# Graph attention, then nucleus diffusion, on one core: the first layer's row work moved between the next chunk's products, and a pair's exponentials placed ahead of a copy-out

## The chip, the core and the metric

The kernel runs on one core of a Trainium2 chip, as one program with one launch. The metric is the device time of the whole program in microseconds (us). Three runs of the kernel before took 3929.79, 3929.95 and 3939.95 us, median 3929.95 us. The profiled execution took 3928.85 us, with a span of 3926.9 us in its trace and a mean granted TensorE clock of 0.938.

The engines are called PE (TensorE: matrix products and transposes), DVE (VectorE), ACT (ScalarE), POOL (GpSimd) and SP (SyncE, which here only issues loads and stores). Each works through its own queue in order.

## The reference, cut to what matters

There are N = 2708 nodes with 512 features, in 22 row tiles of 128 (the last has 20 rows). Everything is float32.

```python
h = relu(layernorm(x))                                    # layer 0: graph attention, 8 heads of 64
feats = einsum('nf,hfd->hnd', h, W)
attn  = softmax(leaky(e_self[:, :, None] + e_neigh[:, None, :]) + mask(adj))
x1    = x + relu(einsum('hnm,hmd->hnd', attn, feats) + b) # heads side by side
v     = relu(layernorm(x1))                               # layer 1: two diffusion steps on v
S = adj + I;  Rf = S by its row sums, Rb = S by its column sums
Xf = Xb = Xa = v;  Z = 0
for s in range(2):
    A  = nucleus_softmax((Xa @ W1) @ W2 @ (Xa @ W3).T)    # per row the largest to 0.9 of the mass
    Xf, Xb, Xa = Rf @ Xf, Rb @ Xb, A @ Xa
    Z += Xf @ U1[s] + Xb @ U2[s] + Xa @ U3[s]
out = x1 + layernorm(v + Z) * gamma + beta
```

(In the reference layer 1 is called with the adjacency matrix as its S.) What matters here: x1 is the output of layer 0; from it come v, the "keys" and "queries" of step 0 (two small projections of v), and a copy of v split into a high and a low part for the products with S.

## The kernel before, in words

**Layer 0.** A first loop over the 22 tiles makes the features `fw`, and the exponentials of the neighbour terms as one row per head, stored in `en_d`. Then the output columns are worked through in six chunks: five of 512 nodes and one of 148. Per chunk, the 22 tiles `a_c` of the transposed adjacency matrix are loaded (L275); ACT sums and converts each (L280) and it is stored into `s_d` as S. For two groups of four heads, and for each of the 22 tiles, DVE makes four tiles `e` (L295, ring of 10) and PE adds each into `po` with one float32 product, which the trace shows as two records (L297). ACT copies the sums to `o_t` (L300). Row sums of the adjacency matrix (`arow`, one buffer, L259 to L260) also run on ACT, four loads per chunk, as early as the buffer allows.

After a chunk's products, each of its tiles is turned back (L313, PE), divided by its sum (L314 to L324, DVE and POOL), gets bias, ReLU and the residual (L325, L326), and is stored as `x1_d` and, with beta added, as `xb_d` (L327 to L329). DVE and PE run this right at the start of the next chunk.

When all chunks are done, W1, W2 and W3 are loaded and combined into `kw` (L351 to L364). Then a loop over 22 tiles (L855 to L864) reloads x1, normalizes it (L137 to L146), clears negatives on POOL (L860) into `va`, splits it (L833, L834, on DVE) into `vhl_d`, turns it on PE (L152), projects it (`project`, L372, eight records per tile), and stores keys and queries in `kq_d` (L378 to L386, ACT and POOL).

Outside the diffusion steps' main part the order of the queues is chosen by the scheduler of the tile framework, from the order of the source and its own estimates.

**Diffusion steps.** In each step (s = 0 and 1) the order on PE, ACT, DVE and SP is the order of the source. Rows are worked in 11 pairs of tiles. `Logits.products` (L440) makes a pair's scores in PSUM, ACT copies them to `p` (L442). `Logits.exp` takes the row maxima (L467, DVE), two exponentials per tile on ACT (L472, L479), a dozen small steps on POOL (`points`, L484 to L495), and 12 passes over `p` on ACT (the "looks", L472). `search` (DVE) narrows the threshold in rounds (L547), calls `early` after its first round and `late` before its last part (`finish`), which makes the kept scores `keep` (L648). Then `attended` turns `keep` on PE (L944) and multiplies by `va` (L963), and `mixed` applies U1, U2, U3 (L991).

S's products run beside this. `part` gives the steps of one half of a quad of tiles: loads of `hl` and `s_r` (L893, L895), products (L899), and at the end `scaled`, which copies the sums out on ACT (L905), stores them, and in step 0 splits them on DVE (L833, L834).

A loop over g from -1 to 10 joins these. At g = -1 nothing can be attended yet. `early` fills the list `fills` with pair 1's exponentials and looks, and `late` runs

```python
paced(others, len(others))     # the second half of S's first products, and their scaled copies
for step in fills:             # then pair 1's exponentials and looks
    step()
```

so that on ACT the exponentials stand behind the copies of S's products. In step 1, `va` is loaded from `xa_d` before everything (L871), and `ranks` counts ties on DVE (L1059) with `spread` (L1065 to L1069) called before the loop.

Of the kernel before, what the change touches and what calls it, by code (L numbers as in the profile page):

```python
# [53 lines left out]
def kernel(  # L54
# [43 lines left out]
    x1_d = dram.tile([N, D], F32, name="x1_d")  # L98

    xb_d = dram.tile([N, D], F32, name="xb_d")  # L100
    y_d = dram.tile([N, D], F32, name="y_d")
# [41 lines left out]
    def layernorm(pool, src, dst, pr):  # L143

        mean, rs = moments(pool, src, pr)
        nc.vector.tensor_scalar(dst, src, mean, rs, op0=OP.subtract, op1=OP.mult)  # L146

    def transposed(pool, psum, src, pr, name):

        pt = psum.tile([P, KD, P], F32, name="t")  # L150
        for k in range(KD):
            nc.tensor.transpose(pt[:, k, :pr], src[:pr, k * P:(k + 1) * P], ident[:pr, :pr])  # L152
        dst = pool.tile([P, KD, P], F32, name=name)
        nc.scalar.copy(dst[:, :, :pr], pt[:, :, :pr])  # L154
        return dst

# [11 lines left out]
    nchunks = [(c, min(c + 512, N)) for c in range(0, N, 512)]  # L168
    with ExitStack() as l0:
# [8 lines left out]
        cpart = big.tile([P, NT, len(nchunks)], F32, name="cpart")  # L178
# [4 lines left out]
        with tc.tile_pool(name="l0w", bufs=1) as wp, tc.tile_pool(name="l0p", bufs=2) as pp, \  # L183
# [9 lines left out]
            for i, vec in enumerate((a_self, a_neigh)):  # L193
                v_b = pp.tile([P, D], F32, name="v_b")
                nc.sync.dma_start(out=v_b, in_=row_bcast(vec, D))
                for k in range(KD):
                    prod = pp.tile([P, D], F32, name="prod")
                    nc.vector.tensor_mul(prod, w_sb[:, k, :], v_b)
                    nc.vector.tensor_reduce(wa[:, k, i * H:(i + 1) * H],
                                            prod.rearrange("p (h d) -> p h d", h=H),  # L200
                                            axis=AX.X, op=OP.add)
            hs = wp.tile([P, KD, NT], F32, name="hs")
            r_t = wp.tile([H, N], F32, name="r_t")
            for t in range(NT):
# [4 lines left out]
                layernorm(pp, xt[:pr], h[:pr], pr)  # L209
# [42 lines left out]
        small = l0.enter_context(tc.tile_pool(name="l0small", bufs=3))  # L252
        ps_o = l0.enter_context(tc.tile_pool(name="l0pso", bufs=6, space=PSUM))
# [10 lines left out]
        for ci, (n0, n1) in enumerate(nchunks):  # L264
            cw = n1 - n0
            tiles = [t for t in range(NT) if n0 <= t * P < n1]
            r_b = rbp.tile([P, H, 512], F32, name="r_b")
            nc.sync.dma_start(
                out=r_b[:, :, :cw],
                in_=bass.AP(tensor=en_d.tensor, offset=en_d.offset + n0, ap=[[0, P], [N, H], [1, cw]]))  # L270
            a_c = []
            for t in range(NT):
# [4 lines left out]
                wide = min(512, NT * P - n0)  # L277
# [8 lines left out]
            for t in tiles:  # L286
                row_sums(t)
            o_t = work.tile([DV, H, 512], F32, name="o_t", bufs=1)
            for grp in hgroups:
                po = [ps_o.tile([DV, 512], F32, name="po") for _ in grp]  # L290
                for t in range(NT):
                    pr = rows[t]
                    for i, hd in enumerate(grp):
                        e = tp.tile([P, 512], F32, name="e")
                        nc.vector.scalar_tensor_tensor(e[:pr, :cw], r_b[:pr, hd, :cw], kk[:pr, t, hd:hd + 1],  # L295
                                                       a_c[t][:pr, :cw], op0=OP.max, op1=OP.mult)
                        nc.tensor.matmul(po[i][:, :cw], lhsT=fw[:pr, t, hd, :], rhs=e[:pr, :cw],  # L297
                                         start=(t == 0), stop=(t == NT - 1))
                for i, hd in enumerate(grp):
                    nc.scalar.copy(o_t[:, hd, :cw], po[i][:, :cw])  # L300
            for t in tiles:
                pr = rows[t]
                c0 = t * P - n0
                xt = work.tile([P, D], F32, name="xt0")
                nc.sync.dma_start(out=xt[:pr], in_=x[cols[t], :])
                o = work.tile([P, D], F32, name="o")
                o3 = o.rearrange("p (h d) -> p h d", h=H)
                den = small.tile([P, H], F32, name="den")
                pos = []
                for g, grp in enumerate(hgroups):  # L310
                    pn = ps_t.tile([P, HG, DV], F32, name=f"pn{g}")
                    for i, hd in enumerate(grp):
                        nc.tensor.transpose(pn[:pr, i, :], o_t[:, hd, c0:c0 + pr], ident[:DV, :DV])  # L313
                    nc.vector.tensor_scalar(den[:pr, grp[0]:grp[-1] + 1], pn[:pr, :, DH],  # L314
                                            lone_n[:pr, t:t + 1], None, op0=OP.add)
                    pos.append(pn)
                rden = small.tile([P, H], F32, name="rden")
                nc.vector.reciprocal(rden[:pr], den[:pr])
                for pn, grp in zip(pos, hgroups):
                    s = slice(grp[0], grp[-1] + 1)  # L320
                    nc.vector.scalar_tensor_tensor(
                        o3[:pr, s, :], fsum.rearrange("p (h d) -> p h d", h=H)[:pr, s, :],
                        lone[:pr, t:t + 1], pn[:pr, :, :DH], op0=OP.mult, op1=OP.add)
                nc.gpsimd.tensor_mul(o3[:pr], o3[:pr], rden[:pr].unsqueeze(2).to_broadcast([pr, H, DH]))  # L324
                nc.gpsimd.tensor_add(o[:pr], o[:pr], b_b[:pr])  # L325
                nc.vector.scalar_tensor_tensor(o[:pr], o[:pr], 0.0, xt[:pr], op0=OP.max, op1=OP.add)  # L326
                nc.gpsimd.dma_start(out=x1_d[cols[t], :], in_=o[:pr])  # L327
                nc.gpsimd.tensor_add(xt[:pr], o[:pr], beta_b[:pr])
                nc.gpsimd.dma_start(out=xb_d[cols[t], :], in_=xt[:pr])  # L329
# [17 lines left out]


    kw = const.tile([P, KD, 2 * DA], F32, name="kw")
    with tc.tile_pool(name="w12", bufs=1) as wp, tc.tile_pool(name="w12ps", bufs=1, space=PSUM) as ps:  # L350
        nc.sync.dma_start(out=kw[:, :, :DA], in_=w3.rearrange("(k p) a -> p k a", p=P))  # L351
        w1_sb = wp.tile([P, KD, DA], F32, name="w1_sb")
        w2_sb = wp.tile([DA, DA], F32, name="w2_sb")
        w1_t = wp.tile([DA, KD, P], F32, name="w1_t")
        nc.sync.dma_start(out=w1_sb, in_=w1.rearrange("(k p) a -> p k a", p=P))
        nc.sync.dma_start(out=w2_sb, in_=w2)
        pw_t = ps.tile([DA, KD, P], F32, name="pw_t")
        for k in range(KD):
            nc.tensor.transpose(pw_t[:, k], w1_sb[:, k], ident)
        nc.scalar.copy(w1_t, pw_t)  # L360
        pw = ps.tile([P, KD, DA], F32, name="pw")
        for k in range(KD):
            nc.tensor.matmul(pw[:, k], lhsT=w1_t[:, k], rhs=w2_sb, start=True, stop=True)
        nc.scalar.copy(kw[:, :, DA:], pw)  # L364

    def project(pool, psum, v_t, t, s):


        pr = rows[t]
        pk = psum.tile([P, KD, P], F32, name="t")  # L370
        for k in range(KD):
            nc.tensor.matmul(pk[:, 0, :pr], lhsT=kw[:, k, :], rhs=v_t[:, k, :pr],  # L372
                             start=(k == 0), stop=(k == KD - 1))
        big = pool.tile([P, P], F32, name="kq_b")
        hl = pool.tile([P, 2, P], F32, name="kq_hl")
        if pr < P:
            nc.gpsimd.memset(hl, 0.0)
        nc.scalar.copy(hl[:, 1, :pr], pk[:, 0, :pr])  # L378
        nc.scalar.mul(big[:, :pr], pk[:, 0, :pr], 4097.0)


        high, x = hl[:, 0, :pr], hl[:, 1, :pr]
        nc.gpsimd.tensor_tensor(high, big[:, :pr], x, op=OP.subtract)
        nc.gpsimd.tensor_tensor(high, big[:, :pr], high, op=OP.subtract)
        nc.gpsimd.tensor_tensor(x, x, high, op=OP.subtract)
        nc.gpsimd.dma_start(out=kq_d[s][:, :, t * P:(t + 1) * P], in_=hl)  # L386
# [440 lines left out]
    def split_rows(pool, x, t, to):  # L827

        pr = rows[t]
        hl = pool.tile([P, 2, D], F32, name="split_hl")  # L830
        if pr < P:
            nc.vector.memset(hl, 0.0)
        nc.vector.tensor_scalar(hl[:pr, 0].bitcast(I32), x.bitcast(I32), -4096, None, op0=OP.bitwise_and)  # L833
        nc.vector.tensor_tensor(hl[:pr, 1], x, hl[:pr, 0], op=OP.subtract)  # L834
        nc.gpsimd.dma_start(out=to[t * P:(t + 1) * P], in_=hl)

    for s in range(STEPS):
        last = s == STEPS - 1
        with ExitStack() as st:
# [14 lines left out]
            if not last:  # L854
                for t in range(NT):  # L855
                    pr = rows[t]
                    x1 = work.tile([P, D], F32, name="yo")
                    nc.sync.dma_start(out=x1[:pr], in_=x1_d[cols[t], :])
                    layernorm(small, x1[:pr], va[:pr, t, :], pr)
                    nc.gpsimd.tensor_scalar(va[:pr, t, :], va[:pr, t, :], 0.0, None, op0=OP.max)  # L860
                    split_rows(parts, va[:pr, t, :], t, vhl_d)
                    v_t = transposed(work, ps_t, va[:, t, :], pr, "v_t")
                    project(small, ps_t, v_t, t, s)
# [4 lines left out]
            rank = big.tile([P, N], BF16, name="rank") if last else None  # L868
            if last:
                for t in range(NT):  # L870
# [294 lines left out]
```

## Time and profile before

The span by stage, read with the view of busy time by windows:

| stage | from, to (us) | what sets its end |
|---|---|---|
| features | 0 to 190 | PE, ACT, POOL in turn |
| chunks 0 to 4, 512 wide | 190 to 997 | PE, about 163 us for a chunk |
| chunk 5, 148 wide | 997 to 1067 | PE and DVE |
| last rows, kw, normalize and project | 1067 to 1237 | a chain over POOL, DVE, PE, ACT |
| step 0 up to the first attended pair | 1237 to 1391 | see the prediction |
| step 0, 11 pairs | 1391 to 2475 | PE |
| step 1 up to the first attended pair | 2475 to 2702 | see the prediction |
| step 1, 11 pairs | 2702 to 3927 | PE |

PE is busy for 3436.3 us of the span, DVE for 2647.5, ACT for 1530.8 and POOL for 792.2. In a timeline row the columns are start, length, engine, line, operation, output and inputs, count; the bracket says how long the engine stood idle before the row and what ended that. A window row gives each engine's busy time in that stretch, then the granted PE clock, the DMA share and GB/s.

### The profile page before, as it was taken

The numbers are of one execution on the slowest core, as the hardware profiler recorded it, in microseconds if no ns is written. First come the engines' busy times: TensorE is split into PE (matmuls) and PEld (weight loads), VectorE is DVE, ScalarE is ACT, GpSimd is POOL, SyncE is SP. The second block draws the span as 40 slices with busy tenths as digits, with TensorE's granted clock in tenths as the row PEclk, the third lists the DMA queues.
The fourth block names the chain that finished last, engine by engine and source line by source line (L and its number), as shares of the span: only waits on it lengthen the run. The fifth ranks groups of instructions, "written<-read, shape, count | busy, mean of one in ns | idle before, by whom it ended". The sixth has DMA issues, their size and how long they took to land. (4 is left out here: it accounts for less than half of the span.)

```text
span 3926.9 us, 35723 instructions
## 1 busy us (share of the span) xinstructions
PE 3436.3 (88%) x11313; PEld 1789.7 (46%) x11313; DVE 2647.5 (67%) x4839; ACT 1530.8 (39%) x2306; POOL 792.2 (20%) x1183
## 2 busy tenths in 40 slices
PE   7998999999745289898989899775999999999988
PEld 4432333333534255554545444353566555566543
DVE  3388898998843644646464552596779977777992
ACT  1243202011012466564656551217545654445511
POOL 3213111020265102122121211301111212112101
PEclk9999999999856799999999999897999999999999
DMA  2377424231145525355454543781676555676652
GB/s 74 101 261 256 130 72 148 67 102 39 39 159 169 179 97 204 134 172 188 148 178 147 185 152 106 236 266 65 211 244 204 203 196 200 210 235 204 209 191 81
DMA packets 276027, 634.10 MB, mean 161 GB/s; under 512 B 36937, under 2 KB 63453, under 8 KB 272803
## 3 DMA queue, kind: packets, MB, share of 16 engines
q1 hardware_dynamic: 248751, 540.99, 41.9%
q0 software_dynamic: 27024, 90.30, 6.0%
q8 instruction: 91, 1.49, 0.2%
q14 instruction: 161, 1.32, 0.1%
HBM read 509.07 MB, written 122.10 MB: 161 GB/s over the span
## 5 line engine op out<-in xcount | busy, mean ns | idle before, releaser
L963 PE MATMUL a<-va,at 128*128 128x512 f32 (+2 forms) x1936 | 888.3, 597 | 10.4 <-ACT at L948 10.2
L297 PE MATMUL po<-e,fw 128*65 128x512 f32 (+3 forms) x2112 | 838.4, 557 | 22.7 <-DVE e L295 22.5
L899 PE MATMUL q<-hl,s_r 128*128 128x512 f32 x2904 | 819.9, 428 | 34.6 <-DMA s_r<-s_d 34.4
L295 DVE SCALAR_TENSOR_TENSOR e<-r_b,kk,a_c 128x512 f32<-128x512 f32 (+3 forms) x1056 | 756.2, 741 | 98.2 <-PE po L297 25.1
L899 PEld LDWEIGHTS q<-hl,s_r 128*128 128x128 f32 x2904 | 543.3, 189 | 278.9 <-issue 131.8
L472 ACT ACTIVATE junk_a<-p,nth 128x2708 uint8<-128x2708 f32 (+1 forms) x240 | 613.0, 2554 | 90.4 <-POOL nth L492 86.8
L297 PEld LDWEIGHTS po<-e,fw 128*65 128x65 f32 (+1 forms) x2112 | 282.5, 141 | 555.0 <-issue 295.6
L991 PE MATMUL a<-u_k,v_t 128*128 128x512 f32 (+1 forms) x1056 | 491.4, 601 | 20.6 <-ACT xa L971 15.2
L963 PEld LDWEIGHTS a<-va,at 128*128 128x128 f32 (+2 forms) x1936 | 336.3, 186 | 373.9 <-issue 340.1
L547 DVE SCALAR_TENSOR_TENSOR junk<-p,th 128x2708 bf16<-128x2708 f32 (+1 forms) x132 | 402.4, 3049 | 4.0
L440 PE MATMUL t<-keys,q_t 128*128 128x452 f32 x528 | 170.7, 452 | 200.6 <-ACT p L442 184.9
L948 ACT COPY at<-t 128x512 f32<-128x512 f32 (+3 forms) x308 | 140.0, 476 | 439.8 <-PE t L944 439.5
L991 PEld LDWEIGHTS a<-u_k,v_t 128*128 128x128 f32 (+1 forms) x1056 | 188.5, 187 | 240.6 <-issue 186.5
L723 DVE SCALAR_TENSOR_TENSOR keep<-p,th 128x2708 f32<-128x2708 f32 (+1 forms) x44 | 133.4, 3033 | 148.1 <-PE t L944 147.0
L440 PEld LDWEIGHTS t<-keys,q_t 128*128 128x128 f32 x528 | 93.7, 215 | 273.2 <-ACT p L442 242.0
L833 DVE TENSOR_SCALAR split_hl<-xe 128x512 int32<-128x512 int32 (+1 forms) x44 | 19.0, 432 | 267.3 <-ACT xe L905 212.6
L725 DVE MAX8 vn<-keep 128x8 f32<-128x2708 f32 (+1 forms) x66 | 196.8, 2981 | 2.3
L280 ACT ACTIVATE s_c<-a_c 128x512 fp32r<-128x512 f32 (+2 forms) x132 | 76.2, 577 | 256.1 <-DMA a_c<-in_adj_t_dram 115.8
L442 ACT COPY p<-t 128x452 f32<-128x452 f32 (+2 forms) x264 | 133.0, 539 | 108.4 <-PE t L440 72.1
L154 ACT COPY v_t<-t 128x512 f32<-128x512 f32 (+1 forms) x154 | 80.9, 570 | 227.2 <-PE t L152 221.4
L944 PE MATMUL t<-ident,keep 128*128 128x128 f32 (+1 forms) x968 | 147.0, 274 | 24.1 <-DVE keep L675 16.0
L944 PEld LDWEIGHTS t<-ident,keep 128*128 128x128 f32 (+1 forms) x968 | 115.1, 139 | 103.8 <-issue 75.7
(275 smaller groups left out, 3220.2 us busy)
## 6 DMA issues: line engine op xcount, KB each, us to landing
s_r<-s_d SPq DMA_DIRECT2D x330, 256.0 KB
hl<-vhl_d SPq DMA_DIRECT2D x132, 512.0 KB
u_k<-in_L_gnn_U_dram SPq DMA_DIRECT2D x264, 256.0 KB
hl<-fhl_d SPq DMA_DIRECT2D x132, 512.0 KB
hl<-bhl_d SPq DMA_DIRECT2D x132, 512.0 KB
arow<-in_adj_dram SPq DMA_DIRECT2D x21, 1354.0 KB
s_d<-s_c SPq DMA_DIRECT2D x110, 256.0 KB
a_c<-in_adj_t_dram SPq DMA_DIRECT2D x105, 256.0 KB
```

The lines of the kernel that those rows point to most:

```text
L295: nc.vector.scalar_tensor_tensor(e[:pr, :cw], r_b[:pr, hd, :cw], kk[:pr, t, hd:hd + 1], a_c[t][:pr, :cw], op0=OP.max, op1=OP.mult)
L297: nc.tensor.matmul(po[i][:, :cw], lhsT=fw[:pr, t, hd, :], rhs=e[:pr, :cw], start=(t == 0), stop=(t == NT - 1))
L440: nc.tensor.matmul(pl[:, :c1 - c0], lhsT=q[:, i], rhs=self.keys[:, c0:c1], start=(i == 0), stop=(i == 1))
L472: nc.scalar.activation(junk[:pr], self.p[i][:pr], func, **kw)
L547: v.scalar_tensor_tensor(junk_b[:pr], ps_[i][:pr], th, ps_[i][:pr], op0=OP.is_ge, op1=OP.mult, accum_out=dst)
L723: v.scalar_tensor_tensor(keep[i][:pr], ps_[i][:pr], t, ps_[i][:pr], op0=OP.is_lt, op1=OP.mult, accum_out=left[:pr, i:i + 1] if e else None)
L725: v.max(vs, keep[i][:pr])
L899: nc.tensor.matmul(half[j], lhsT=s_r[:, j * P:(j + 1) * P], rhs=hl[:, h], start=(c == 0 and h == 0), stop=(c == NT - 1 and h == 1))
L944: nc.tensor.transpose(pt[:rows[c], j, :pr], keep[i][:pr, cols[c]], ident[:pr, :pr])
L948: nc.scalar.copy(at[:r, j0:j1, :pr], pt[:r, j0:j1, :pr])
L963: nc.tensor.matmul(pa[:pr], lhsT=at[:rows[c], j, :pr], rhs=va[:rows[c], c, :], start=(c == 0), stop=(c == NT - 1))
L991: nc.tensor.matmul(pz[i][:rows[t]], lhsT=v_t[i][:, k, :rows[t]], rhs=u_k, start=(n == 0 and k == 0), stop=(n == 2 and k == KD - 1))
```

## The change

What the change does, in five parts.

1. The tail of layer 0 becomes a list of five stages per tile (`finished`): `turned`, `shared`, `normed`, `cleared`, `asked`. They are kept in `later` and run one per step of the next chunk's first head group: stage n of the i-th tile after tile 5i + n of the loop over 22 tiles. Stages of the last chunk run when all products are done. The layer norm, the split and the projections of v are now in these stages, so x1 is not stored and reloaded, and the loop over 22 tiles before step 0 is gone. v is cleared by ACT (`Relu`), stored to `va_d` and loaded again later; one of the two split operations moves from DVE to POOL; `kw` is made at the very start.
2. Chunks are divided evenly by tiles: 4, 4, 4, 4, 3, 3 (widths 512 four times, 384, 276).
3. The row of neighbour exponentials `r_b` is loaded per head group, half as large.
4. `va` is loaded by `values()` after the first half of S's products is queued, in both steps.
5. At g = -1 the exponentials and looks of pair 1 come ahead of the second half of S's products, and in step 1 `spread` comes ahead of them, inside `late`.

```diff
-    nchunks = [(c, min(c + 512, N)) for c in range(0, N, 512)]
+    tchunks = []                      # 4, 4, 4, 4, 3, 3 tiles
...
+            def turned():
+                nc.sync.dma_start(out=xt[:pr], in_=x[cols[t], :])
+                    pn = ps_t.tile([P, 512], F32, name=f"pn{g}")
+                        nc.tensor.transpose(pns[g][:pr, i, :], o_t[:, hd, c0:c0 + pr], ident[:DV, :DV])
...
+            def shared():             # den, rden, o on DVE; then on POOL:
+                nc.gpsimd.tensor_mul(o3[:pr], o3[:pr], rden[:pr].unsqueeze(2).to_broadcast([pr, H, DH]))
+                nc.gpsimd.tensor_add(o[:pr], o[:pr], b_b[:pr])
+            def normed():
+                nc.vector.scalar_tensor_tensor(o[:pr], o[:pr], 0.0, xt[:pr], op0=OP.max, op1=OP.add)
+                held.extend(moments(small, o[:pr], pr))
+                nc.gpsimd.tensor_add(xt[:pr], o[:pr], beta_b[:pr])
+                nc.gpsimd.dma_start(out=xb_d[cols[t], :], in_=xt[:pr])
+            def cleared():
+                nc.vector.tensor_scalar(o[:pr], o[:pr], mean, rs, op0=OP.subtract, op1=OP.mult)
+                nc.scalar.activation(v[:pr], o[:pr], AF.Relu)
+                nc.gpsimd.dma_start(out=va_d[cols[t], :], in_=v[:pr])
+            def asked():
+                pt = ps_t.tile([P, 512], F32, name="pn0").rearrange("p (k d) -> p k d", k=KD)
+                    nc.tensor.transpose(pt[:, k, :pr], v[:pr, k * P:(k + 1) * P], ident[:pr, :pr])
+                nc.scalar.copy(v_t[:, :, :pr], pt[:, :, :pr])
+                split_rows(halves, nc.gpsimd, v[:pr], t, vhl_d)
+                project(halves, ps_t.tile([P, 512], F32, name="pn1"), v_t, t, 0)
...
+                    for stage in later.pop(t, ()):
+                        stage()
...
+            for i, t in enumerate(tiles):
+                for n, stage in enumerate(finished(t, o_t, t * P - n0)):
+                    later.setdefault(i * 5 + n, []).append(stage)
+        for n in sorted(later):
+            for stage in later[n]:
+                stage()
...
-            if not last:
-                for t in range(NT):
-                    nc.sync.dma_start(out=x1[:pr], in_=x1_d[cols[t], :])
-                    layernorm(small, x1[:pr], va[:pr, t, :], pr)
-                    nc.gpsimd.tensor_scalar(va[:pr, t, :], va[:pr, t, :], 0.0, None, op0=OP.max)
-                    split_rows(parts, va[:pr, t, :], t, vhl_d)
-                    v_t = transposed(work, ps_t, va[:, t, :], pr, "v_t")
-                    project(small, ps_t, v_t, t, s)
...
-                if last:
-                    spread()
+                values()              # 22 loads of va, 256 KB each
...
+                        elif last:
+                            spread()
+                        if g < 0:
+                            paced(fills, len(fills))
                         paced(others, len(others))
-                        for step in fills:
-                            step()
+                        paced(fills, len(fills))
```

## The prediction

> **What bounds the kernel now.** I read the busy time by engine first, then the 40 slices for where PE is not busy, then busy time by windows there, and last the timeline for what ends each wait.
>
> ```profile
> PE 3436.3 (88%) x11313; PEld 1789.7 (46%) x11313; DVE 2647.5 (67%) x4839; ACT 1530.8 (39%) x2306; POOL 792.2 (20%) x1183
> ...
> PE   7998999999745289898989899775999999999988
> ```
>
> PE sets the time, and the change adds or removes almost no product. So what it can move is PE's idle time, which lies in the dips of the second line.
>
> ```profile
> 833.00:997.00 164.00, 158.63 (x386) 50.86 (x384) 145.11 (x209) 14.22 (x52) 28.42 (x39) 0.98 0.15 45
> 997.00:1067.00 70.00, 58.86 (x389) 43.78 (x389) 67.36 (x193) 2.30 (x9) 18.57 (x20) 0.88 0.12 43
> 1067.00:1237.00 170.00, 70.48 (x289) 57.38 (x289) 63.18 (x127) 23.47 (x70) 115.95 (x186) 0.52 0.42 142
> 1237.00:1391.00 154.00, 67.34 (x248) 46.20 (x248) 89.78 (x176) 76.25 (x88) 22.89 (x47) 0.74 0.50 170
> 2475.00:2702.00 227.00, 126.41 (x467) 87.08 (x466) 160.59 (x272) 82.35 (x107) 39.71 (x49) 0.80 0.66 219
> ```
>
> A window row gives start:end, length, then busy time of PE, PEld, DVE, ACT, POOL, the granted clock, DMA share, GB/s. A full chunk (833 to 997) is PE's with 5 us to spare; DVE is close behind. The last rows (1067 to 1237) have no busy engine but POOL, 116 of 170 us. The two starts (1237 to 1391 and 2475 to 2702) have PE idle for 87 and 101 us. The timeline says why:
>
> ```profile
> 1187.80 1.11 PE L152 MATMUL t<-ident,va 128*128 128x128 f32 x4 [6.30 <-POOL va L860]
> 1189.64 2.08 PE L372 MATMUL t<-v_t,kw 128*128 128x128 f32 x8 [0.73 <-ACT v_t L154]
> ...
> 1309.40 0.69 ACT L905 ACTIVATE xe<-q,rinv 128x512 f32<-128x512 f32 x1 [25.19 <-PE q L899]
> 1333.87 2.55 ACT L472 ACTIVATE junk_a<-p,nmx 128x2708 uint8<-128x2708 f32 x1
> 1382.69 0.95 ACT L442 COPY p<-t 128x452 f32<-128x452 f32 x2
> ...
> 2641.79 1.27 ACT L905 ACTIVATE xe<-q,cinv 128x512 f32<-128x512 f32 x2 [58.45 <-PE q L899]
> 2647.20 2.55 ACT L472 ACTIVATE junk_a<-p,nmx 128x2708 uint8<-128x2708 f32 x1
> 2694.57 0.74 PE L440 MATMUL t<-keys,q_t 128*128 128x452 f32 x1 [50.67 <-ACT p L442]
> ```
>
> In step 1 ACT stood idle for 58 us in front of the copy of S's sums (L905), with pair 1's exponentials queued behind it; PE then waited 50.67 us for ACT.
>
> **What the Trainium skill says.** "TensorE: Matmul & The Clock Gate", section "What's actually happening": an idle PE falls to about half its clock. The trace agrees: at a clock of 0.52 eight products of `project` took 2.08 us, and 1.16 in one warmer case. "GPSIMD Engine Reference", section "1. Specifications": POOL shares its SBUF access with DVE and contends with DVE instructions that read two inputs from SBUF. The trace agrees: a tiny POOL operation took 0.20 us at 1348 and 2.69 at 2535, under DVE's passes:
>
> ```profile
> 1348.37 0.20 POOL L486 TENSOR_TENSOR x<-x 128x2 f32<-128x2 f32 x1
> 2535.60 2.69 POOL L486 TENSOR_TENSOR x<-x 128x2 f32<-128x2 f32 x1
> 388.21 10.09 POOL L261 TENSOR_SCALAR lone<-rsum 128x1 f32<-128x1 f32 x1 [8.46 <-ACT arow L260]
> ```
>
> The third row is the worst case: a one-column operation took 10.09 us under the `e` stream. `e` is such a two-input operation, so this is what the moved POOL work meets.
>
> **Part 1 and 2, in the chunks.** By the timeline the chunks end at 506.5, 669.7, 833.2, 997.2 and 1067.3. A product shows as two records of 0.43 us at 512 columns and 0.141 at 148, so 0.322 and 0.232 at 384 and 276 (interpolated). A full chunk is 8 x 22 x 2 = 352 records, 151.4 us. Each moved tile adds on PE four transposes of v (0.5), the products of `project` warm (1.0), beside its turning (0.66) that is there already: 2.2 us. It adds on DVE bn 0.66 + 0.17, subtract 0.55 and the mask 0.42 to the 2.0 us already there: 3.8 us.
> Between two stages of a chunk lie four `e` of 0.71 us, so a tile (five stages) has 20 x 0.71 = 14.2 + 3.8 = 18.0, with waits of some 1.5 about 19.5 on DVE, against 40 x 0.43 + 2.2 = 19.4 on PE: even. POOL's work is about 9.6 us per tile, half its time if unhindered.
> - Chunk 0: `r_b` halved; the first `e` waited 6.65 us for its loads. About -3.
> - Chunk 1: 8 row sums (`arow`) of 9.5 us stand on ACT among the stages. A stage that wants v or v_t from ACT then holds PE. I take 3 + 6 + 6 + 3 = 18 us, an estimate from a half to two thirds of one row sum for each tile. 151.4 + 4 x 2.2 + 9 (first turning behind `arow`; the trace had 8.79) + 18 + 2 = 189 against 174.6: +14.5.
> - Chunks 2 and 3: 151.4 + 8.8 + 2.3 = 162.5 against 163.1 and 163.8: -2.
> - Chunks 4 and 5: 352 x 0.322 + 8.8 + 2.3 = 124.4, and 352 x 0.232 + 8.8 + 4.5 = 95; together 219 against 234: -15. The 148-wide chunk cost more than its columns: 70 us where 352 x 0.141 is 50.
>
> Sum about -5: last product near 1063.
>
> **Part 1, the tail.** 170 us of chain over 22 tiles go; left are three tiles (the last chunk's) after the last product, and they are serial, since pn0 and pn1 have one buffer each and both are used at the start and the end of a tile. From the trace one tile's chain (turn, shares, POOL's product and sum, layer norm, v, turn, project, split) is 13.1 us: 39.3, then POOL's last part 1.9, the write of kq 2.2, the load of keys 2.5, after which only the last columns of pair 0's scores are left: 46 us, so its `p` is complete near 1063 + 46 = 1109. Before, it was complete at 1244.3. **-135**.
>
> **Part 4 and 5, step 0.** Pair 0's p ready, S's products run at some 290 GB/s of loads (768 KB for each 2.65 us), so the 22 loads of va, 5.55 MB or 20 us, push the last of them from 1309 to 1331 (times here on the old clock, with scores at 1237). ACT now does exponentials (10.6 us), points, 12 looks (31.9) from 1297 on: end 1347.6. The scaled copies follow, 1347.6 to 1366, because each waits for DVE's splits and their stores; DVE's last split moves from 1337.6 to 1366.7; behind it stands `finish`, 29.6 us by the trace: 1396.3 against 1391.1. **+5**: the copies, once ahead of `finish`, are now behind the looks. The va loads are under this.
>
> **Part 4 and 5, step 1.** The loads of va (2485 to 2501) stood ahead of q_t; PE waited 15.38 us for keys and 6.54 for q_t. That chain moves some 6 us to the front. The exponentials no longer wait for the sums at 2641.8: ACT, idle from 2583, ends them near 2590; POOL's points, under DVE's counts at 2.6 us each, end near 2612; 12 looks end near 2645 and the copies near 2650, instead of 2693.9. There are no splits in this step, so DVE's `finish` does not wait; it ended at 2665, goes to 2659 with the front. PE's first turning (L944) goes from 2702 to 2661. **-38**, DVE's next search (waiting for looks until 2695) gains 34, so I take a little less than PE's 41.
>
> **Costed at nothing.** `kw` at the start: PE is idle until 27.4 us there, waiting for h. The clear moved to ACT (14 us busy in 164). The split's subtraction on POOL: in POOL's 9.6. `spread` in `late`: DVE has it either way ahead of `finish`.
>
> Sum: -135 + 5 - 38 = **-168**; 3930 - 168 = **3762 us**.
>
> **Where a wait is added.** `shared` and `cleared` on DVE wait for PE and POOL, `asked` on PE for ACT. Behind them are `e` and products; the ring of ten `e` holds 2.5 rounds, 7 us of DVE's work, in which PE can go on. That is why a POOL chain of 1 to 6 us costs little if a whole group of `e` lies between stages.
>
> **Rivals.**
> (A) The stages do not hide: each of 19 tiles costs 6 us more (1.2 us per stage, the gap of one late POOL result). For it: DVE and PE are even, so nothing absorbs. Against: DVE does its stage after four `e`, and runs ahead. 3762 + 114 = 3876. Chance 0.12.
> (B) Step 1 gains nothing because DVE's `finish` and its POOL steps, not ACT, last longest: 3762 + 38 = 3800. For it: POOL's 2.6 us steps. Against: the 50.67 us wait ends at ACT. Chance 0.15.
> (C) The loads of va land on the path of S's products, +20: 3782. For: DMA is at 290 GB/s there. Against: ACT's looks end later. Chance 0.08.
> (D, slower) POOL starves as in the 10.09 us row, once per tile: 19 x 10 = 190: 3952. For: that row. Against: other small POOL rows in the stream have 0.2 to 0.8 us. Chance 0.06.
> The forecast itself: 0.59.
>
> **How the numbers follow.** The likeliest gives 3762. Downward: ACT's 18 us in chunk 1 may be nothing, and step 0's +5 and the tail's serial 13 us per tile may overlap by 20: 3720. Upward the range takes in B and C, to 3815; A and D, 0.18, are left out. Faster 0.91 (all but D and a part of A with more than the 6 us), same 0.02, slower 0.07.
>
> **What would show it.** In the profile after: last product (L297) near 1063 and pair 0's `p` complete near 1109; PE's idle time in chunk 1 ended by ACT; full chunks of 162 to 163 us; L472 ahead of L905 at both starts; from there to step 0's first L944 about 152 us, where before it was 1244.3 to 1391.1, 146.8 us; and in step 1 the stretch from its first scores to L944 some 38 us shorter. Wrong if chunks 2 and 3 take over 170 us with idle ended by DVE or POOL, or if the wait at L944 is for DVE.

## The result, and the profile after

The kernel after takes 3808.18 us (median of 4 runs, 3805.34 to 3809.46), beside 3929.87 us for the kernel before in the same comparison: ratio 0.9685, 95% interval 0.9667 to 0.9704. That is 122 us less. The prediction was 3762 us (168 less), with a range of 3720 to 3815. The direction and most of the mechanism were right; 46 us of the forecast gain did not come.

First the page of the kernel after: busy time by engine, and PE in 40 slices.

```profile
PE 3402.3 (89%) x11313; PEld 1772.6 (47%) x11313; DVE 2611.5 (69%) x4814; ACT 1542.6 (41%) x2328; POOL 825.6 (22%) x1186
...
PE   7999999999955398999989899769999999999888
```

PE executes the same 11313 instructions as before. The first dip (the last rows of layer 0, and step 0's start) is narrower, and so is the second (step 1's start). What is left of them, and the two narrow chunks, in the view of busy time by windows of the kernel after:

```profile
847.80:982.70 134.90, 125.41 (x433) 54.63 (x432) 127.95 (x225) 20.55 (x65) 55.16 (x72) 0.99 0.31 101
982.70:1082.20 99.50, 90.60 (x405) 51.98 (x403) 92.17 (x194) 7.59 (x19) 31.11 (x39) 0.98 0.12 44
1082.20:1140.40 58.20, 17.42 (x75) 13.10 (x75) 12.50 (x36) 8.00 (x20) 29.08 (x41) 0.53 0.33 100
1140.40:1301.80 161.40, 65.57 (x235) 45.86 (x234) 86.60 (x174) 73.13 (x82) 22.15 (x45) 0.71 0.57 201
2314.20:2578.00 263.80, 195.88 (x673) 109.25 (x673) 155.95 (x257) 91.45 (x134) 55.93 (x64) 0.90 0.62 202
```

In the narrow chunks (first two rows) DVE is busier than PE, which it is in no 512-wide chunk (in chunk 2 DVE has 149 us and PE 164). The tail (third row) has no engine busy for more than half of it. Its granted clock is 0.53, as the Trainium skill's section named in the prediction ("TensorE: Matmul & The Clock Gate", "What's actually happening") has it for an idle PE, and eight products of `project` take up to 2.08 us there, where they take 1.05 to 1.16 in most of the chunks' stages. The fifth row begins at the last attended pair of step 0, so it has more PE work than the row of step 1's start shown before.

Cut at the same events in both traces (last product L297 / L413; `p` of the first tile complete, which is where DVE's first row maximum starts; first turning of `keep`, L944 / L983; the last pair's first turning in step 0), the span divides as follows, in us:

| stretch | before | after | change | predicted |
|---|---|---|---|---|
| start to last product | 1067.3 | 1082.3 | +15.0 | -5 |
| to first `p` complete | 177.0 | 58.1 | -118.9 | -130 |
| to step 0's first turning | 146.8 | 161.5 | +14.7 | +5 |
| to step 0's last pair | 1012.0 | 1012.3 | +0.3 | 0 |
| to step 1's first turning | 299.1 | 263.9 | -35.2 | -38 |
| to the end | 1224.7 | 1226.9 | +2.2 | 0 |
| sum | 3926.9 | 3804.9 | -122.0 | -168 |

So the miss is 20 us in the chunks, 11 in the tail, 10 at step 0's start, and 5 in the rest. The timeline of the kernel after shows what ends the waits now; the rows answer to those shown of before:

```profile
1091.64 1.12 PE L373 MATMUL pn<-ident,v 128*128 128x128 f32 x4 [8.57 <-ACT v L366]
1093.48 2.08 PE L160 MATMUL pn<-v_t,kw 128*128 128x128 f32 x8 [0.73 <-ACT v_t L375]
1121.68 0.61 PE L373 MATMUL pn<-ident,v 20*128 20x20 f32 x4 [10.37 <-ACT v L366]
1134.69 5.00 PE L496 MATMUL t<-keys,q_t 128*128 128x452 f32 x12 [10.14 <-DMA q_t<-kq_d]
...
1239.39 0.67 ACT L944 ACTIVATE xe<-q,rinv 128x512 f32<-128x512 f32 x1
1293.16 0.97 ACT L498 COPY p<-t 128x452 f32<-128x452 f32 x2 [29.73 <-DVEq L863]
1301.85 1.14 PE L983 MATMUL t<-ident,keep 128*128 128x128 f32 x8
...
2557.26 1.27 ACT L944 ACTIVATE xe<-q,cinv 128x512 f32<-128x512 f32 x2 [13.53 <-PE q L938]
2569.17 0.97 ACT L498 COPY p<-t 128x452 f32<-128x452 f32 x2 [6.88 <-DVEq L863]
2569.76 8.14 PE L496 MATMUL t<-keys,q_t 128*128 128x452 f32 x20 [10.34 <-ACT p L498]
2578.05 1.14 PE L983 MATMUL t<-ident,keep 128*128 128x128 f32 x8
```

The 50.67 us wait of PE in step 1 is 10.34 us now, and ACT waits there until DVE has passed a branch (L863, where `finish` decides which arm to run), not for S's sums. The reason can be read in the source: ACT is about to copy the next pair's scores into `p`, which has four buffers, two for a pair, and `finish` may still read the two that are written next. In step 0 ACT is done early and waits 29.73 us for that branch. In both steps the next pair's scores (L496, some 8 us) stand on PE between the branch and the first turning.

### The profile page after: what moved, and what is told of

Read it like the earlier page. It is cut to its first block, busy times and chain, and to the rows that moved or that the text cites. A ratio compares the mean times of both kernels' runs of the same rounds, so it can differ in the third digit from the quotient of the medians.

```text
span 3804.9 us, 35734 instructions
## 1 busy us (share of the span) xinstructions
PE 3402.3 (89%) x11313; PEld 1772.6 (47%) x11313; DVE 2611.5 (69%) x4814; ACT 1542.6 (41%) x2328; POOL 825.6 (22%) x1186
## 5 line engine op out<-in xcount | busy, mean ns | idle before, releaser
L413 PE MATMUL po<-e,fw 128*65 128x512 f32 (+4 forms) x2112 | 841.1, 554 | 29.9 <-DVE e L411 17.3
L411 DVE SCALAR_TENSOR_TENSOR e<-r_b,kk,a_c 128x512 f32<-128x512 f32 (+4 forms) x1056 | 752.5, 741 | 68.7 <-PE po L413 18.9
L413 PEld LDWEIGHTS po<-e,fw 128*65 128x65 f32 (+1 forms) x2112 | 286.4, 140 | 545.1 <-issue 272.9
L496 PE MATMUL t<-keys,q_t 128*128 128x452 f32 x528 | 168.1, 447 | 167.0 <-ACT p L498 155.0
L496 PEld LDWEIGHTS t<-keys,q_t 128*128 128x128 f32 x528 | 92.6, 213 | 237.9 <-ACT p L498 208.0
L395 ACT ACTIVATE s_c<-a_c 128x512 fp32r<-128x512 f32 (+3 forms) x132 | 76.2, 577 | 253.1 <-DMA a_c<-in_adj_t_dram 129.4
L983 PE MATMUL t<-ident,keep 128*128 128x128 f32 (+1 forms) x968 | 147.3, 274 | 24.3 <-DVE keep L731 16.6
L983 PEld LDWEIGHTS t<-ident,keep 128*128 128x128 f32 (+1 forms) x968 | 115.1, 139 | 104.2 <-issue 75.9
L523 DVE TENSOR_REDUCE nmx<-p 128x1 f32<-128x2708 f32 (+1 forms) x44 | 129.2, 2966 | 26.7 <-ACT p L498 26.7
```

The source lines that it names most:

```text
L411: nc.vector.scalar_tensor_tensor(e[:pr, :cw], r_b[:pr, i, :cw], kk[:pr, t, hd:hd + 1], a_c[t][:pr, :cw], op0=OP.max, op1=OP.mult)
L496: nc.tensor.matmul(pl[:, :c1 - c0], lhsT=q[:, i], rhs=self.keys[:, c0:c1], start=(i == 0), stop=(i == 1))
L983: nc.tensor.transpose(pt[:rows[c], j, :pr], keep[i][:pr, cols[c]], ident[:pr, :pr])
```

## The experiments

Each is the kernel after (3808) with the edit named, timed beside the kernel before. Times move by a few us from run to run: in kernels with an identical layer 0 it ended between 1079.6 and 1085.2, and their chunk 2 took 167.3 in one trace and 170.1 in another. So an edit is read from the stretch that it touches, in the trace, and the total second. Times within a stretch come from the traces, cut as in the table above.

### Step 1: the order alone

```diff
-                        if g < 0:
+                        if g < 0 and not last:
                             paced(fills, len(fills))
```

> The kernel after, with the old order in step 1 alone. Theory: the order brought nearly all of the 35 us of this start: 3840. Rival: the later loads of va brought it: 3808 to 3814.

Measured 3847.93 us, ratio 0.9785 (0.9763 to 0.9806): 40 us slower than the kernel after. S's sums are copied at the same time (2557.60 here, 2557.26 there), and the first turning is at 2618.20 in place of 2578.05. The old wait is back, in the timeline of this kernel:

```profile
2610.00 6.68 PE L496 MATMUL t<-keys,q_t 128*128 128x452 f32 x16 [50.29 <-ACT p L498]
```

With the old order step 1's start (as cut in the table) takes 304.7 us, beside 299.1 in the kernel before and 263.9 in the kernel after. So the gain comes with the order: the later loads of va and the moved `spread` bring none of it by themselves. Whether they add to it under the new order was not run.

### Step 0: the order, the loads of va, and a third order

The order as before in step 0:

```diff
-                        if g < 0:
+                        if g < 0 and last:
                             paced(fills, len(fills))
```

> The kernel after, with the old order (S's copies, then exponentials and looks) in step 0 alone. Theory 1, the loads of va delay S's products by some 15 us, so the old order is as late as the new one: 3808, within 4. Theory 2, the new order alone costs the 15 us that step 0's start is longer (157.6 against 142.1 us): 3793.

Measured 3798.29 us, 0.966 (0.9633 to 0.9687). From the second tile's row maximum to the first turning it takes 151.6 us; the kernel after takes 157.6, the kernel before 142.0. So neither theory holds alone. With the old order PE waits for ACT's looks, as before:

```profile
1290.76 1.50 PE L496 MATMUL t<-keys,q_t 128*128 128x452 f32 x3 [71.31 <-ACT p L498]
```

But S's products end some 10 us later than in the kernel before, behind the loads of va. The new order costs another 6 on top of that.

The new order, with the loads of va behind S's products:

```diff
-                values()
+                if last:
+                    values()
...
                         paced(others, len(others))
+                        if g < 0 and not last:
+                            values()
```

> The kernel after, with only the loads of va in step 0 behind S's products; the new order stays. Theory 1 (the looks hold the copies until their end in any case): 3808, within 3. Theory 2 (the loads of va alone cost the 15 us): 3793.

Measured 3803.76 us, 0.9679 (0.9663 to 0.9696); the same stretch takes 157.7 us, no change. PE now ends S's products some 11 us sooner, but the copies stand behind the looks and start no sooner. In the new order the loads of va cost nothing, as the prediction said; they cost some 10 us only in the old one, by the comparison with the kernel before.

A third order, with the copies between exponentials and looks (one look still stands ahead of them) and va behind S's products:

```diff
                         if g < 0:
-                            paced(fills, len(fills))
+                            paced(fills, len(fills) if last else len(fills) - 12)
                         paced(others, len(others))
+                        if g < 0 and not last:
+                            values()
                         paced(fills, len(fills))
```

> The kernel after, with step 0 alone in a third order: exponentials, then S's copies, then the 12 looks, and the loads of va behind S's products. Theory: DVE's splits of S's sums, which the copies release, stand ahead of its last part (25.8 us) and of the p copies (8.5 us); with the copies ahead of the looks and S's loads not behind va, the start of step 0 is 126 us instead of 157.6: -31, 3777. Rival: ACT's looks, not DVE, end last: no more than -10, 3798.

Measured 3778.54 us, 0.9612 (0.9596 to 0.9628). The stretch takes 131.4 us in place of 157.6. In the timeline of this kernel, ACT waits only 2.18 us for DVE's branch where it waited 29.73, because DVE's splits are over sooner and its last part runs under the looks:

```profile
1232.74 2.54 ACT L528 ACTIVATE junk_a<-p,nth 128x2708 uint8<-128x2708 f32 x1
1238.45 3.03 DVE L779 SCALAR_TENSOR_TENSOR keep<-p,th 128x2708 f32<-128x2708 f32 x1
1264.33 0.97 ACT L498 COPY p<-t 128x452 f32<-128x452 f32 x2 [2.18 <-DVEq L863]
```

Step 0's start is a matter of two chains that both leave ACT: the looks, behind which only the next pair's scores stand, and the copies, behind which DVE's last splits and `finish` stand, some 29 us from the last copy to the branch. In this order the copies fall between the exponentials and all looks but one, and the 29 us run beside the looks: both end near 121 us of the stretch. That the copies are ahead is not enough (they are in the old order too, with the exponentials behind them). The late loads of va are in the run before too (157.7 us), so the order brings all of the 26 us; what the early loads would take from it was not run.

### The chunks: POOL's sums

Leaving out the bias b and the addition of beta in the stages, two of POOL's four wide operations (the output lacks both):

```diff
-                nc.gpsimd.tensor_add(o[:pr], o[:pr], b_b[:pr])
...
-                nc.gpsimd.tensor_add(xt[:pr], o[:pr], beta_b[:pr])
-                nc.gpsimd.dma_start(out=xb_d[cols[t], :], in_=xt[:pr])
+                nc.gpsimd.dma_start(out=xb_d[cols[t], :], in_=o[:pr])
```

> The kernel after, leaving out two of POOL's four wide operations per tile in the stages: the bias b and the addition of beta (so the output lacks both). Theory: POOL's wide sums and DVE's e hold each other up, and DVE waits 1.2 us for the bias sum; without them 2.3 us less per tile where DVE sets the pace, and about 2.5 us less per tile in the tail: -24 - 7 = -31, 3777. Rival: POOL is not what slows the first halves: only the tail's -7, 3801.

Measured 3773.62 us, 0.9599 (0.9583 to 0.9616): 35 less. The last product is at 1051.4 in place of 1082.3; the tail is 2.3 shorter, less than expected. From chunk to chunk (first turning to first turning) the time in us is:

| chunk | 1 | 2 | 3 | 4 (384) | 5 (276) |
|---|---|---|---|---|---|
| predicted | | 162.5 | 162.5 | 124.4 | 95 |
| kernel after | 170.7 | 167.3 | 167.7 | 135.0 | 99.5 |
| without the two sums | 167.9 | 161.1 | 161.9 | 127.9 | 93.5 |

In chunks 2 and 3 together PE waits 6.3 us for `e` in the kernel after (12 times), and not once without the two sums; in chunks 4 and 5 it waits 10.6 us for `e`, and 2.2 without. DVE does the same work in both: in chunk 4 its `e` are busy for 117.1 us with the sums and 111.4 without, and its waits for POOL or for the DMA that POOL issues fall from 3.4 to 1.2 us. So most of the 7.1 us there are `e` that took longer. One can see it row by row. DVE of the kernel after, in chunk 4, while POOL works on the product and the bias of one tile (868.27 to 871.15) and on beta (872.25 to 873.83):

```profile
868.11 3.46 DVE L411 SCALAR_TENSOR_TENSOR e<-r_b,kk,a_c 128x384 f32<-128x384 f32 x3
...
872.09 0.60 DVE L411 SCALAR_TENSOR_TENSOR e<-r_b,kk,a_c 128x384 f32<-128x384 f32 x1
...
873.22 1.01 DVE L411 SCALAR_TENSOR_TENSOR e<-r_b,kk,a_c 128x384 f32<-128x384 f32 x1
...
874.25 0.58 DVE L411 SCALAR_TENSOR_TENSOR e<-r_b,kk,a_c 128x384 f32<-128x384 f32 x1
```

An `e` alone is 0.60 us. Three of them took 3.46 beside the product and the bias, where three alone take 1.8 at most, and one took 1.01 beside beta. The same place without the two sums (only the product is left):

```profile
864.71 1.92 DVE L409 SCALAR_TENSOR_TENSOR e<-r_b,kk,a_c 128x384 f32<-128x384 f32 x2
...
867.16 0.61 DVE L409 SCALAR_TENSOR_TENSOR e<-r_b,kk,a_c 128x384 f32<-128x384 f32 x1
...
868.29 0.59 DVE L409 SCALAR_TENSOR_TENSOR e<-r_b,kk,a_c 128x384 f32<-128x384 f32 x1
```

The prediction took the contention of DVE and POOL one way only, POOL slowed by DVE. It goes the other way too, and there it lands on the engine that paces the chunk.

Moving beta out of the stages, into the second head group, in the source (`o`, which it reads, gets four buffers and is no longer overwritten):

```diff
-                nc.gpsimd.tensor_add(xt[:pr], o[:pr], beta_b[:pr])
+            def based():                  # a sixth stage, at NT + 1 + 5 * i
+                nc.gpsimd.tensor_add(xt[:pr], o[:pr], beta_b[:pr])
```

> The kernel after, with POOL's addition of beta moved out of the stages to the second head group of the chunk (for the last chunk, to the very end); nothing on DVE waits for it. Theory: POOL's wide sums slow DVE's e, so moving one of the two left out before brings about half of the 28 us of the chunks, and 1.9 us for each of three tiles in the tail: -14 - 5.5, 3789. Rival: what counted there was DVE's own wait for the bias sum: only the tail's -5.5, 3802.

Measured 3814.31 us, 0.97 (0.9687 to 0.9713): no gain, if anything slower. The edit did not do what it was meant to do. POOL's order here is the scheduler's, and it put the sums where POOL was free, in the middle of the stages and three close together. POOL's timeline in this kernel, chunk 2:

```profile
562.04 1.71 POOL L380 TENSOR_TENSOR xt<-o,beta_b 128x512 f32<-128x512 f32 x1 [0.80 <-DVE o L356]
566.45 1.68 POOL L380 TENSOR_TENSOR xt<-o,beta_b 128x512 f32<-128x512 f32 x1 [0.69 <-DMA xb_d<-xt]
571.67 1.47 POOL L380 TENSOR_TENSOR xt<-o,beta_b 128x512 f32<-128x512 f32 x1
```

So it says nothing about a sum in the second half of a chunk; that remains untried.

### The chunks: where the stages stand

The stages every second step over both head groups (the sums `o_t` of the first group need a second buffer):

```diff
-                    for stage in later.pop(t, ()):
+                    for stage in later.pop(gi * NT + t, ()):
...
-                    later.setdefault(i * 5 + n, []).append(stage)
+                    later.setdefault(i * 10 + 2 * n, []).append(stage)
```

> The kernel after, with the five stages of a tile every second step over both head groups of the next chunk instead of every step of the first (the first head group's sums get a second buffer). Theory: in the first half of a chunk DVE has e (0.71 us at 512, 0.60 at 384), 3.8 us of stages per tile, some 2 us lost to POOL's wide sums and 2 us of waits, so DVE sets the pace there and PE in the second half. Spread out, chunks 2 and 3 go from 167 to 163, chunk 4 from 136 to 132, chunk 1 by 3: about -16, 3792. Rival: every stage holds PE by its own wait wherever it stands: 3808, no change.

Measured 3799.16 us, 0.9655 (0.9633 to 0.9678). The chunks took 169.0, 172.7, 173.8, 128.4 and 94.0 us: chunks 4 and 5 were 6 us shorter each, chunks 2 and 3 longer. The same kernel once more:

> The kernel with the stages over both head groups once more, since its trace showed chunks 2 and 3 at granted clocks of 0.94 and 0.96 (0.98 in the kernel after) and 5 to 6 us longer, chunks 4 and 5 6 us shorter. If the clock was chance, chunks 2 and 3 are now at or under 167 us and the time is near 3793; if spreading itself makes 512-wide chunks slower, they stay at 172 and the time at 3800.

Measured 3795.42 us, 0.9654 (0.9641 to 0.9668). Chunks 1 to 5 took 171.9, 167.4, 172.7, 128.6 and 93.7 us. The narrow chunks gain again, more than first expected (6.4 and 5.8): there DVE set the pace in the first half, and PE's waits for `e` fall from 10.6 to 3.2 us. In the wide ones these waits go from 6.3 us to none, but nothing is gained. Chunk 2's 172.7 was not repeated, and its granted clock was 0.94 then and 0.97 now. Chunk 3 has a cause that the trace shows, a new wait of PE:

```profile
828.55 2.08 PE L160 MATMUL pn<-v_t,kw 128*128 128x128 f32 x8 [8.61 <-ACT v_t L375]
```

ACT's copy of v_t stood behind its sums of the next chunk's adjacency tiles (L395), which came with gaps of 3 to 10 us in that stretch, some of them waits for their loads. In the first half of a chunk there are almost none of these in its queue. Chunk 2 has the same wait, of 2.71 us; why else it stays at 167 in place of 163 was not settled.

Chunks of 4, 4, 4, 4, 4 and 2 tiles, as before:

```diff
-        tchunks.append(list(range(t0, t0 + NT // NB + (c < NT % NB))))
+        tchunks.append(list(range(t0, min(t0 + TG, NT))))
```

> The kernel after, with chunks of 4, 4, 4, 4, 4, 2 tiles as before. By the runs so far: chunk 4 167 us, chunk 5 (148 wide) with four staged tiles of some 13 us each about 87, together +18 against 136 + 100; the tail has two tiles, -14.6: 3812. By the prediction's own numbers (even chunks save 15, one more tile in the tail costs 13): 3810. If the even division is worth more than that, over 3820.

Measured 3801.84 us, 0.9674 (0.9658 to 0.969): not slower, perhaps 4 us faster. The last product is 11.3 us later and the tail, with two tiles, 15.0 shorter (43.1). So the even division costs what it brings; the 15 us that the prediction gave it in the chunks are spent again on the third tile of the tail.

### The tail

The last chunk's three tiles stage by stage, not tile by tile, with PSUM from the finished products' banks and three buffers for the tiles that the stages hand on:

```diff
-                    pn = ps_t.tile([P, 512], F32, name=f"pn{g}")
+                    pn = bank(f"pn{g}")           # last chunk: ps_o.tile(..., name="po")
...
-                    later.setdefault(i * 5 + n, []).append(stage)
+                    later.setdefault(n * len(tiles) + i if tiles is tchunks[-1] else i * 5 + n, []).append(stage)
```

> The kernel after, with the stages of the last chunk's three tiles interleaved (stage by stage, PSUM from the six banks of the finished products, three buffers). Theory: the 58 us from the last product to the first p are a serial chain of 13.1 + 14.6 + 14.7 us because a tile must end before the next begins; interleaved, POOL's 9.5 us per tile set it: -13, 3795. Rival: the loads of keys and queries or POOL set it already: less than 4 us, 3805.

Measured 3800.99 us, 0.9669 (0.9646 to 0.9691). PE ends the third tile's `project` at 1106 in place of 1124.6 in the kernel after, but the tail is only 5.7 us shorter (52.4). In POOL's timeline of this kernel the third tile now waits for buffers:

```profile
1112.60 0.94 POOL L180 MEMSET split_hl<- 128x1024 f32 x1 [2.05 <-DMA vhl_d<-split_hl]
1117.42 0.31 POOL L164 MEMSET kq_hl<- 128x256 f32 x1 [3.88 <-DMA kq_d<-kq_hl]
```

The split and the keys of the stages have one buffer each, and it comes free only when its store has landed. These waits, 5.9 us, would account for most of the 7 us that did not come, but later runs bear that out only in part. In the last kernel below, with two buffers for the keys, the last store of keys is issued 31.0 us after the last product (40.4 here, 45.1 in the kernel after). The tail still takes 50.8 us. The load behind that store is issued 5.8 us after it there and 1.6 here, and the loads of the queries then wait another 3.8 us for the store of the split, which still has one buffer. With two buffers for both, and beta out of the tail, it takes 48.5 (the first kernel below). So when the stages end sooner, the stores behind them are what comes last; why the store of the keys takes longer there was not settled.

### Edits together

Four edits: the third order in step 0, the tail with two buffers for the split and the keys, and beta as above.

> The kernel after, with four edits together: step 0's copies between exponentials and looks and va behind S's products (-26), the last chunk's stages interleaved (-7), two buffers for the split and the keys of the stages in place of one (-3), beta in the second head group (-14, and some of the tail's 5.5): if they add up 3757; if the tail's edits overlap, 3764.

Measured 3777.20 us, 0.9608 (0.9595 to 0.9621), no better than the third order alone. The tail is 48.5 us, 9 less than in the run with the third order, but the last product is 9.9 later: with the moved sums of beta the chunks took back what the tail gave (chunk 4 took 138.9 us here).

Then only what had gained: the third order, the tail with two buffers for the keys, and the spread stages in the two narrow chunks (three buffers in place of four for the converted adjacency tiles make room). TG is 4, so a chunk's tiles are spread where the next chunk has three:

```diff
-                    later.setdefault(i * 5 + n, []).append(stage)
+                    later.setdefault(n * len(tiles) + i if tiles is tchunks[-1] else i * 5 + n if len(tchunks[ci + 1]) == TG else i * 10 + 2 * n, []).append(stage)
```

> The kernel after, with what gained alone: step 0's copies between the exponentials and looks and va behind S's products (-26 in its stage), the last chunk's stages interleaved with two buffers for the keys (-7 to -10), and the stages spread over both head groups only in the two narrow chunks (-12 by the traces of the spread kernel). If they add up: 3808 - 26 - 8 - 12 = 3762. If the tail's gain or the spreading is lost beside the others: 3775.

Measured 3759.90 us (3755.63 to 3761.93), 0.9571 (0.9558 to 0.9584), 48 us below the kernel after. By the trace the last product is 13.8 us earlier, the tail 7.3 shorter, and step 0's start 27.1 shorter: they add up to 48.2.

## Why the prediction was right and where it was not

- **What bounds the kernel, and the rows that go.** Right. The chain over 22 tiles is gone, and PE has the same work.
- **The part "in the chunks", chunk 1.** Right in direction, the term of 18 us for row sums ahead of the stages on ACT was too large: chunk 1 took 170.7 us from its first turning, which leaves 8.5 for it beside the 162.2 of the other terms. Chunks 0 and 1 ended at 512.8 against 518 in the sum. The 9 us for the first turning were close: PE waited 6.47 us for ACT there.
- **The same part, chunks 2 to 5: wrong by 25 us.** The failed step is "about 19.5 on DVE, against 19.4 on PE: even", with waits of 1.5 and `e` at their undisturbed 0.71. The later tiles took 21.3 us in chunk 2 (546.2 to 567.5) and 18.5 in chunk 4, where PE needs 40 x 0.322 + 2.2 = 15.1 by the prediction's own numbers and DVE was not worked out at all. There 20 `e` of 0.60 and 3.8 us of stages are 15.8; without two of POOL's sums such a tile took 16.6, so 1.9 of the 2.7 us between come with these sums. The run without them takes back 25 us in these four chunks. Two slips in the sum are smaller: chunk 5 has the stages of three tiles and not four, so its 95 should have been 92.8; and the record times called interpolated are 0.43 in proportion to the columns, which the kernel after bears out (0.32 to 0.33 and 0.23 to 0.25 in the long rows).
- **The tail: mis-sized, 58.1 against 46.** The stages took 45.1 us up to the last issue of a store, not 41.2: the first tile took the 13.1 of the sum, but in the next two POOL first finished the keys of the tile before, and for the short third one cleared a buffer. From there the sum had 4.7 us; it took 13.0. After the issue of the last keys' store it took 3.0 us until the load behind it was issued, 4.4 from there to the first product with the queries, whose loads stand behind those of the keys in SP's queue, and the first tile's scores were not mostly done before but all made after (1134.69 to 1140.3).
- **Step 0: +5 forecast, +14.7 measured.** The chain was right: copies behind the looks, DVE's splits behind the copies, `finish` behind the splits. On the clock of before the branch comes at 1397.1, and the sum said 1396.3. The failed step is to end the sum at the branch: behind it come the next pair's scores and copies, 8.7 us, which before lay behind the looks and now lie behind the branch.
- **Step 1: -38 forecast, -35.2 measured.** Right, and the run with the old order loses 40 us. The scores behind the branch were left out here as well. ACT went on from the branch 255.0 us after the last pair's first turning of step 0, where the sum had DVE done after 255.9; but the first turning of step 1 came 8.9 us behind that, and the sum had 2. That the forecast is so near is in part luck: 3 of PE's 41 us were taken off for another reason.
- **Work costed at nothing.** `kw` at the start and the clearing on ACT did hide. The split on POOL did not quite: in chunk 4 seven `e` beside it and the keys' small sums took 5.40 us, where seven alone take 4.2.
- **The rivals.** A (a stall for each stage, 3876) did not come, but some of it did, more from contention than from late results. B (step 1 gains nothing) did not come, though DVE does come last there now. C (va on the path) holds for the old order only, with some 10 us and not 20. D (POOL starved, 3952) did not come: POOL's wide operations took 1.0 to 1.7 us in the chunks' stages.
- **Its own sign of being wrong.** It named a wait at the first turning (L944) that is for DVE. In both steps that is how the chain now ends, at DVE's branch. But in the prediction's own sums `finish` comes last in both steps too (1396.3 and 2659), so this sign contradicts its working and does not speak against the mechanism.

The Trainium skill's section on shared SBUF access ("GPSIMD Engine Reference", "1. Specifications") was read as a risk to POOL. The runs fit the same sharing seen from DVE's side, with 3.46 us for three `e` in place of 1.8.

## What to carry to other kernels

When work is moved under a stretch that an engine paces, add up every engine's time over the part of the stretch where it goes, not over the whole, and count what the moved work does to the pacing engine's own operations. When a wait is removed, follow the queue past it to what comes next: here 8.7 us of scores stood behind a branch that had not been last at this place before. And of two pieces that two chains wait for on one engine, put first the one with the more work behind it on other engines: here the copies, with some 29 us of DVE's work.

## What was not expected of the hardware

A wide two-input sum on POOL (1.3 to 1.7 us) lengthens the `e` that DVE runs at the same time: one of 0.60 us took 1.01 beside beta, and three took 3.46 beside the product and the bias; leaving out two sums per tile gave back 28 us in five chunks. And DVE-to-POOL contention was milder in the stages than the 10.09 us row suggested: no wide sum of POOL there took over 1.71 us.
